# Token places in the rows, scattered block results, rows loaded by register address, and projections moved ahead of the dispatch

## The chip, the cores and the metric

The kernel runs on one core of a Trainium2 chip. The metric is the device time of one execution in microseconds (us); smaller is better. A core has TensorE (PE in the profile, its weight loads PEld), VectorE (DVE), ScalarE (ACT), GpSimd (POOL), SyncE (SP) and 16 DMA engines. On a profile's lines "L336" is line 336 of the kernel.

## The reference, cut to what matters

Three layers over x of 8 items, each 256 channels by 1024 positions, all in fp32:

```python
# layer 0: attention over each item's 1024 positions, 8 heads of 64, with a residual
qkv = (xt @ w_qkv + b_qkv).reshape(B, S, N_HEADS, 3 * D_K)
q, k, v = jnp.split(qkv, 3, axis=-1)
attn = softmax(einsum('bihd,bjhd->bijh', q, k) * SCALE, axis=1)   # over i, so each j is a column
res = einsum('bijh,bjhd->bihd', attn, v) @ w_out + b_out + xt
# layer 1: layer norm, then an attention of one head with one matrix W on the normed
#          tokens n (scores n W n^T, softmax, times n), added to the tokens
# layer 2: n = layer norm of the tokens; mixture of experts, 8 experts, the best 2 per token
probs = softmax(n @ router_w.T); rw, re = top_k(probs, 2); rw = rw / rw.sum(-1)
out = n
for e in range(8):
    h = gelu(n @ w1[e] + b1[e]); y = h @ w2[e] + b2[e]
    out = out + combine[:, e:e+1] * y      # combine holds rw at the chosen experts, else 0
# the tokens are added, and the result is returned as 8 x 256 x 32 x 32
```

A token's result therefore needs the rows of its two experts. The kernel computes only those, in sorted order.

## The kernel before, in words

**One item at a time.** For item b, `layer0` makes v for all positions (`values`, pv, L291) and q and k by head pair (`project`, pqk, L272, evicted by VectorE as qk, L280). It then runs 32 steps: four head pairs times eight column tiles. A step scores two heads on TensorE (psc, L323), takes the negative maximum on VectorE (nmax, L334), the exponential on ScalarE (ex, L336), scales the values on VectorE (rs L343, vs L345), and two steps later sums values on TensorE (po, L361). The next pair's projections are laid at column tiles 3 and 5. Then come the output projection (pr, L400 and L404) and t1 (L407). `attend` is the second layer: layer norm n1, transposes pt_n (L215), px (L421), scores ps (L436), transposes pa (L453), py (L458) and t2 (L463).

**Dispatch.** `dispatch` normalises t2 into n2, transposes it (pt_n, L215) and computes the router's scores pl (L482). Some 50 small VectorE operations choose the two best experts per token and count, with two small matmuls (pc L562, pn L564), at which row of its expert's region a token goes. For each 128 tokens and each of the two choices POOL then scatters 128 rows of 256 floats into `rows` in DRAM (L610): 16 indirect DMAs per item. POOL adds n2 to t2 (L617) and SP stores that as `sums` (L618).

The tiles n1, n2 and, later, `total` share the tag "n", which has one buffer: the next of them is written only when the last reader of the one before is done.

**Experts.** Items 0 to 6 are one group, item 7 is the second. When a group is dispatched, `plan` works out on VectorE which expert each block of 256 rows has, where its rows start (row_at), where its weights are (w_at) and at which place of y each token's two results will stand (yat). `experts` then runs 63 blocks for the first group, 15 for the second, in three staggered stages: `fetch` gathers weights (wb, L715, three buffers) and rows (xr, L724, three buffers) by POOL's indirect DMAs, and transposes the rows (px L733, xb L735); `hidden` is the first matrix and gelu (ph L743, hb L753); `collect` is the second matrix (pe L768), the bias (yb L777) and a store of the block to y by SP (L782).

**Results.** `results` loads an item's sums into `total` (o, L796), gathers for each 128 tokens the two rows of y by POOL (yk, L800, four buffers), adds them times their gates on VectorE (o, L806), transposes (pout, L817), copies on ScalarE and stores.

**Order.** The order on each engine is decided by a scheduler that goes by the order of the program and by what is ready in its own estimate; at run time each engine works in that fixed order. The program before:

```python
        for g in waiting:
            experts(g)
            for at, item in enumerate(g.items):
                between[at * NPAIR // len(g.items)].append((g, item))
        t1 = layer0(b, xT, between)
        t2 = attend(b, t1)
        dispatch(b, t2, group)
```

So the first group's blocks stand ahead of layer0(7), its results are spread between the head pairs of layer0(7), and experts(1) and results(7) end the kernel. At the start, while item 0 runs, SP fills `rows` with zeros and packs the weights (`prepare`).

Of the kernel before, what the change touches and what calls it, by code (L numbers as in the profile page):

```python
# [10 lines left out]
F32 = mybir.dt.float32  # L11
I32 = mybir.dt.int32
AF = mybir.ActivationFunctionType
ALU = mybir.AluOpType
AX = mybir.AxisListType
# [3 lines left out]
def kernel(  # L19
# [21 lines left out]
    nc = tc.nc  # L41
    P = 128
# [12 lines left out]
    BR = R * P  # L55
    WROW = NCC * FF + NFC * D + NFC + D
# [68 lines left out]
    for e in range(E):  # L125
# [15 lines left out]
    r_iota = const.tile([P, 1], F32, name="r_iota")  # L141
    nc.gpsimd.iota(
        r_iota, [[1, 1]], base=0, channel_multiplier=R, allow_small_or_imprecise_dtypes=True
# [74 lines left out]
    def prepare():  # L218

        zero = wbs[0][:, : 2 * D]  # L220
        with tc.issue_after(evicted[0, 0, 1].ins):
            nc.vector.memset(zero, 0.0)

        def fill(group):

            per = E * group.cap // (2 * P)
            return [
                nc.sync.dma_start(
                    group.rows.rearrange("(p c r) d -> p c (r d)", p=P, r=2)[:, c : c + 32],
                    zero.unsqueeze(1).to_broadcast([P, 32, 2 * D]),  # L230
                )
                for c in range(0, per, 32)
            ]

        first = fill(groups[0])[0]
        with tc.issue_after(first.ins):
            pack()
            for group in groups[1:]:
                fill(group)
# [62 lines left out]
    def layer0(b, xT, between):  # L302
# [4 lines left out]
        v = values(b, xT)  # L307
        res = one.tile([P, NPAIR, S], F32, tag="res", name=f"res_{b}")
        qks = [[project(b, xT, 0, t) for t in range(2)]]
        if b == 0:  # L310
            prepare()
# [61 lines left out]
        for at in range(last + LAG + 1):  # L373
            if at <= last:
                score(at, 0, 0)
            if 0 < at <= last + 1:
                score(at - 1, 1, 1)
                soften(at - 1, 1)
            if at <= last:
                score(at, 0, 1)  # L380
                score(at, 1, 0)
                soften(at, 0)
            if at >= LAG:
                gather_values(at - LAG)
            if at <= last:
                g, j = steps[at]
                if j == NT - 1:
                    for group, item in between[g]:
                        results(group, [item])
                if g + 1 < NPAIR and j in (3, 5):  # L390
                    if j == 3:
                        qks.append([])
                    qks[g + 1].append(project(b, xT, g + 1, len(qks[g + 1])))
# [17 lines left out]
    def attend(b, t1):  # L411
        n1 = one.tile([P, NT, D], F32, tag="n", name=f"n1_{b}")
# [64 lines left out]
    def gates(b, nT):  # L477

        pl = acc(f"pl_{b}")
        for i in range(NT):  # L480
            for dc in range(NCC):
                nc.tensor.matmul(  # L482
                    pl[:, ts(i, E)],
                    nT[:, dc, ts(i, P)],
                    rT[:, dc, :],
                    start=(dc == 0),
                    stop=(dc == NCC - 1),
                )

# [40 lines left out]
    class Group:  # L530


        def __init__(self, n, items):
            self.n, self.items = n, items
            self.cap = len(items) * S
            self.nb = 2 * self.cap // BR + E - 1
            self.rows = dram.tile([E * self.cap, D], F32, name=f"rows_{n}")
            self.views = dram_disjoint_views(self.rows, 2 * NT * len(items))
            self.y = dram.tile([self.nb * BR, D], F32, name=f"y_{n}")
            self.sums = [dram.tile([P, NT, D], F32, name=f"sums_{b}") for b in items]  # L540
            self.counts = None
            self.kept = {}
# [3 lines left out]
    def dispatch(b, t2, group):  # L546

        n2 = one.tile([P, NT, D], F32, tag="n", name=f"n2_{b}")
# [3 lines left out]
        gate, hots = gates(b, nT)  # L552
# [38 lines left out]
        kept = []  # L591
        for k in range(2):
# [3 lines left out]
            row = keep.tile([P, NT], F32, tag=f"row{k}", name=f"row{k}_{b}")  # L596
            nc.vector.tensor_reduce(row, sel, AX.X, ALU.add)  # L597
            nc.vector.tensor_mul(sel, hot, e_iota.unsqueeze(1).to_broadcast([P, NT, E]))
            exp = keep.tile([P, NT], F32, tag=f"exp{k}", name=f"exp{k}_{b}")
            nc.vector.tensor_reduce(exp, sel, AX.X, ALU.add)  # L600
            to = small.tile([P, NT], F32, tag="d_to", name=f"d_to_{b}_{k}", bufs=2)
# [3 lines left out]
            kept.append((row, exp, at))  # L605
        for i in range(NT):
            for k in range(2):
                at = kept[k][2]
                view = group.views[2 * (NT * group.items.index(b) + i) + k]
                nc.gpsimd.indirect_dma_start(  # L610
                    out=view[:, :],
                    out_offset=bass.IndirectOffsetOnAxis(ap=at[:, i : i + 1], axis=0),
                    in_=n2[:, i, :],
                    in_offset=None,
                )

        nc.gpsimd.tensor_add(t2, t2, n2)  # L617
        nc.sync.dma_start(group.sums[group.items.index(b)], t2)  # L618
        group.kept[b] = gate, [(row, exp) for row, exp, _ in kept]

    def plan(group):
# [23 lines left out]
        first = keep.tile([P, E], F32, tag="first", name=f"first_{n}", bufs=2)  # L645
# [7 lines left out]
        e_of = tmp("p_e", [nb])  # L653
# [10 lines left out]
        nc.vector.tensor_scalar(base, first, -float(BR), r_iota, ALU.mult, ALU.add)  # L664
# [5 lines left out]
        nc.vector.tensor_scalar_min(lo, lo, float(cap - R))  # L670
# [13 lines left out]


        for b in group.items:
            gate, kept = group.kept[b]
            ats = []
            for k, (row, exp) in enumerate(kept):
                hot = small.tile([P, NT, E], F32, tag="d_sel", name=f"p_hot_{b}_{k}", bufs=1)  # L690
                nc.vector.tensor_tensor(
                    hot,
                    exp.unsqueeze(2).to_broadcast([P, NT, E]),
                    e_iota.unsqueeze(1).to_broadcast([P, NT, E]),
                    ALU.is_equal,
                )
                nc.vector.tensor_mul(
                    hot, hot, first.unsqueeze(1).to_broadcast([P, NT, E])
                )
                to = small.tile([P, NT], F32, tag="d_to", name=f"p_to_{b}_{k}", bufs=2)  # L700
                nc.vector.tensor_reduce(to, hot, AX.X, ALU.add)
                nc.vector.scalar_tensor_tensor(to, to, float(BR), row, ALU.mult, ALU.add)
                at = keep.tile([P, NT], I32, tag=f"yat{k}", name=f"yat{k}_{b}")
                nc.vector.tensor_copy(at, to)
                ats.append(at)
            group.kept[b] = gate, ats
        return row_at, w_at

    def experts(group):
        n = group.n  # L710
        row_at, w_at = plan(group)

        def fetch(b):
# [9 lines left out]
            xr = rowp.tile([P, R, D], F32, tag="xr", name=f"xr_{n}_{b}")  # L723
            nc.gpsimd.indirect_dma_start(  # L724
                out=xr.rearrange("p r d -> p (r d)"),
                out_offset=None,
                in_=group.rows[:, :],
                in_offset=bass.IndirectOffsetOnAxis(ap=row_at[:, b : b + 1], axis=0),
# [7 lines left out]
            return xb  # L736

        def hidden(b, xb):
# [21 lines left out]
            return hT  # L760

        def collect(b, hT):
# [19 lines left out]
            nc.sync.dma_start(group.y[ts(b, BR), :].rearrange("(p r) d -> p r d", r=R), yb)  # L782

        line = [None, None]
        for b in range(group.nb + 2):
            if line[1] is not None:
                collect(*line[1])
            line[1] = (line[0][0], hidden(*line[0])) if line[0] is not None else None
            line[0] = (b, fetch(b)) if b < group.nb else None

    def results(group, items):
        for b in items:
            gate, ats = group.kept[b]
            sums = group.sums[group.items.index(b)]
            total = one.tile([P, NT, D], F32, tag="n", name=f"o_{b}")
            nc.sync.dma_start(total, sums)  # L796
            for i in range(NT):
                for k in range(2):
                    yk = four.tile([P, D], F32, tag="yk", name=f"yk{k}_{b}_{i}")
                    nc.gpsimd.indirect_dma_start(  # L800
                        out=yk[:, :],
                        out_offset=None,
                        in_=group.y[:, :],
                        in_offset=bass.IndirectOffsetOnAxis(ap=ats[k][:, i : i + 1], axis=0),
                    )
                    nc.vector.scalar_tensor_tensor(  # L806
                        total[:, i, :],
                        yk,
# [12 lines left out]

    waiting = []
    for b in range(B):
# [4 lines left out]

        between = [[] for _ in range(NPAIR)]
        for g in waiting:  # L830
            experts(g)
            for at, item in enumerate(g.items):
                between[at * NPAIR // len(g.items)].append((g, item))
        t1 = layer0(b, xT, between)
        t2 = attend(b, t1)
        dispatch(b, t2, group)
# [46 lines left out]
```

## Time and profile before

| what | value |
|---|---|
| median of 15 runs | 2924.97 us (2908.84 to 2943.03) |
| the profiled execution | 2926.14 us, span 2924.4 us |
| mean granted TensorE clock | 0.943 |
| TensorE matmuls | 2629.4 us, 90% |
| TensorE weight loads | 1373.6 us, 47% |
| VectorE | 1480.2 us, 51% |
| ScalarE | 844.1 us, 29% |
| POOL | 443.1 us, 15% |
| POOL's scatters of rows (L610) | 128, mean 977 ns |
| POOL's gathers: yk (L800), wb (L715), xr (L724) | 128 of 966 ns, 78 of 1015 ns, 78 of 963 ns |
| data moved by DMA | 209.17 MB |

The span is the time from the first to the last instruction of the profiled execution; its whole time is 1.7 us longer. Busy times are sums over the span, so an engine at 51% may still set the pace in one stage. A line of a timeline gives the start, the duration, the engine, the line, the operation with the tiles it writes and reads, and in brackets how long the engine stood idle before and what ended that. In the table of waits the three numbers are the total, the number of times and the longest, in us. In the table by stretches each row has the window, its length, the busy time and count for TensorE, its weight loads, VectorE, ScalarE and POOL, then the granted clock, the DMA share and GB/s.

### The profile page before, as it was taken

The page shows a single profiled execution, that of the slowest core. Times are in us where ns is not written, and L with a number is a line of the kernel's source. Part 1 is how long each engine was busy: PE and PEld are TensorE (multiplying, and loading weights), DVE is VectorE, ACT ScalarE, POOL GpSimd, SP SyncE. Part 2 cuts the span into 40 slices and gives each one's busy share as a digit, 9 for nine tenths or more (in the row PEclk, how much of TensorE's full clock was granted, in tenths as well). Part 3 has the DMA queues.
Part 4 walks back from the last instruction along what each step waited for, and adds up shares of the span by engine and source line. Part 5 has one row for each costly group of instructions (what it writes and reads, how often), then busy time and mean ns, then how long its engine had stood idle before and what let it go on. Part 6 is the DMA issues. An engine that isn't in the chain of part 4 may idle for free.

```text
span 2924.4 us, 26495 instructions
## 1 busy us (share of the span) xinstructions
PE 2629.4 (90%) x10049; PEld 1373.6 (47%) x10049; DVE 1480.2 (51%) x2666; ACT 844.1 (29%) x1451; POOL 443.1 (15%) x445
## 2 busy tenths in 40 slices
PE   8999999999999999999999998999499988878946
PEld 3346434633464346434643464346377752224634
DVE  4664566456645664565456545664433335545422
ACT  2531253125312531154125412531011113323101
POOL 0000200020002000200020002000444442441043
PEclk9999999999998999899999999999699998879968
DMA  6983100010001000100010001000355532332044
GB/s 246 385 301 127 58 1 15 1 44 1 15 1 44 1 15 1 43 1 15 0 44 1 15 0 44 1 1 1 121 176 186 183 98 80 111 94 69 0 169 156
DMA packets 89304, 209.17 MB, mean 72 GB/s; under 512 B 16256, under 2 KB 22040, under 8 KB 87128
## 3 DMA queue, kind: packets, MB, share of 16 engines
q1 hardware_dynamic: 59272, 128.87, 12.1%
q0 software_dynamic: 29904, 78.61, 8.4%
q8 instruction: 79, 1.29, 0.2%
q14 instruction: 49, 0.40, 0.0%
HBM read 113.22 MB, written 126.36 MB: 82 GB/s over the span
## 4 chain that ended last, share of the span: by engine, by line
PE 73%; issue 16%; DVE 6%; ACT 3%; DMA 2%; POOL 1%; another core or an unknown queue 0%; ACTq 0%; SPq 0%; DVEq 0%; POOLq 0%
PE psc L323 18%; PE po L361 15%; PE py L458 8%; PE ps L436 7%; PE pqk L272 6%; PE pr L400 4%; PE pe L768 3%; PE ph L743 2%; PE pt_n L215 2%; PE px L421 2%; PE pa L453 2%; PE pv L291 2%; DVE nmax L334 1%; ACT ex L336 1%; PE pl L482 1%
## 5 line engine op out<-in xcount | busy, mean ns | idle before, releaser
L336 ACT ACTIVATE ex<-psc,nmax 128x1024 f32<-128x1024 f32 x512 | 570.7, 1115 | 880.3 <-DVE nmax L334 729.1
L334 DVE TENSOR_REDUCE nmax<-psc 128x1 f32<-128x1024 f32 x512 | 604.1, 1219 | 261.6 <-PE psc L323 222.8
L323 PE MATMUL psc<-qk,qk 64*128 64x512 f32 x2048 | 615.9, 642 | 48.9 <-DVE qk L280 25.7
L361 PE MATMUL po<-ex,vs 128*64 128x512 f32 x2048 | 513.2, 618 | 15.2 <-DVE vs L345 14.7
L323 PEld LDWEIGHTS psc<-qk,qk 64*128 64x128 f32 x2048 | 234.7, 190 | 396.6 <-ACT ex L336 171.2
L617 POOL TENSOR_TENSOR t<-t,n 128x2048 f32<-128x2048 f32 x8 | 36.1, 4511 | 1907.9 <-issue 1500.3
L361 PEld LDWEIGHTS po<-ex,vs 128*64 128x64 f32 x2048 | 128.0, 138 | 371.6 <-issue 308.3
L272 PE MATMUL pqk<-xT,wqkv 128*128 128x512 f32 x512 | 239.5, 614 | 12.5 <-ACT ex L336 10.7
L458 PE MATMUL py<-n,aT 128*128 128x256 f32 x1024 | 236.5, 384 | 11.2 <-DVE aT L455 11.2
L436 PE MATMUL ps<-nT,xa 128*128 128x512 f32 x512 | 236.8, 592 | 0.0
L458 PEld LDWEIGHTS py<-n,aT 128*128 128x128 f32 x1024 | 190.4, 190 | 67.4 <-DVE aT L455 43.8
L280 DVE TENSOR_SCALAR qk<-pqk,b_qk 128x1024 f32<-128x1024 f32 x64 | 82.2, 1284 | 200.1 <-PE pqk L272 191.7
L272 PEld LDWEIGHTS pqk<-xT,wqkv 128*128 128x128 f32 x512 | 95.6, 194 | 156.5 <-issue 110.7
L768 PE MATMUL pe<-wb,hb 128*128 128x256 f32 x624 | 155.2, 392 | 13.6 <-ACT hb L753 8.4
L447 ACT ACTIVATE ex<-ps,nmax 128x1024 f32<-128x1024 f32 x64 | 71.3, 1115 | 332.8 <-DVE nmax L444 325.1
L800 POOL DMA_INDIRECT yk<-y,yat x128 | 123.7, 966 | 204.1 <-DVE o L806 109.1
L743 PE MATMUL ph<-xb,wb 128*128 128x256 f32 x624 | 151.4, 386 | 3.2 <-DVE xb L735 3.1
L610 POOL DMA_INDIRECT rows<-n,d_at x128 | 125.0, 977 | 170.5 <-DVE row L597 118.4
L753 ACT ACTIVATE hb<-ph,wb 128x256 f32<-128x256 f32 x156 | 65.5, 471 | 282.0 <-issue 241.1
L463 DVE SCALAR_TENSOR_TENSOR t<-py,rs,t 128x256 f32<-128x256 f32 x64 | 31.0, 484 | 228.2 <-PE py L458 228.2
L291 PE MATMUL pv<-wqkv,xT 128*128 128x512 f32 x256 | 135.0, 677 | 9.0 <-ACT wqkv L95 7.2
L735 DVE COPY xb<-px 128x512 f32<-128x512 f32 x78 | 54.0, 692 | 157.0 <-PE px L733 101.0
(151 smaller groups left out, 2332.9 us busy)
## 6 DMA issues: line engine op xcount, KB each, us to landing
rows<-wb SPq DMA_DIRECT2D x8, 8192.0 KB
y<-yb SPq DMA_DIRECT2D x78, 256.0 KB
sums<-t SPq DMA_DIRECT2D x8, 1024.0 KB
o<-sums SPq DMA_DIRECT2D x8, 1024.0 KB
out_dram<-oT SPq DMA_DIRECT2D x16, 512.0 KB
xT<-in_x_dram SPq DMA_DIRECT2D x7, 1024.0 KB
wpack<-in_L_ffn_w_dram SPq DMA_DIRECT2D x4, 1024.0 KB
rows<-n,d_at POOLq DMA_INDIRECT x128
```

The costliest lines, as they stand in the source:

```text
L272: nc.tensor.matmul(pq[:, ts(n, 512)], wqkv[:, cc, t, ts(g, P)], xT[:, cc, ts(n, 512)], start=(cc == 0), stop=(cc == NCC - 1),)
L291: nc.tensor.matmul(pv[:, ts(j, 512)], xT[:, cc, ts(i + j, P)], wqkv[:, cc, 2, :], start=(cc == 0), stop=(cc == NCC - 1),)
L323: nc.tensor.matmul(pss[at, h][:, ts(n, 512)], k[r, ts(j, P)], q[r, ts(n, 512)], start=True, stop=True)
L334: nc.vector.tensor_reduce(nmax, ps, AX.X, ALU.max, negate=True)
L336: nc.scalar.activation(ex, ps, AF.Exp, bias=nmax, scale=1.0, accum_out=sums[at][:, h : h + 1])
L361: nc.tensor.matmul(po[n][h * DK : (h + 1) * DK, :], vs[:, h, :], exs[h][:, ts(n, 512)], start=(j == 0), stop=(j == NT - 1),)
L436: nc.tensor.matmul(psc[:, ts(n, 512)], xa[:, ec, ts(i, P)], nT[:, ec, ts(n, 512)], start=(ec == 0), stop=(ec == NCC - 1),)
L458: nc.tensor.matmul(py[:, :D], aT[:, ts(m, P)], n1[:, m, :], start=(m == 0), stop=(m == NT - 1))
L610: nc.gpsimd.indirect_dma_start(out=view[:, :], out_offset=bass.IndirectOffsetOnAxis(ap=at[:, i : i + 1], axis=0), in_=n2[:, i, :], in_offs ...
L743: nc.tensor.matmul(ph[:, ts(fc, BR)], wb[:, dc * FF + fc * P : dc * FF + (fc + 1) * P], xb[:, dc, :], start=(dc == 0), stop=(dc == NCC - 1),)
L768: nc.tensor.matmul(py[:, ts(r, D)], hT[:, fc, ts(r, P)], wb[:, at + fc * D : at + (fc + 1) * D], start=(fc == 0), stop=(fc == NFC - 1),)
L800: nc.gpsimd.indirect_dma_start(out=yk[:, :], out_offset=None, in_=group.y[:, :], in_offset=bass.IndirectOffsetOnAxis(ap=ats[k][:, i : i + ...
```

## The change

Four things are changed together.

1. A row in `rows` is 260 floats, not 256: column 256 holds the token's place (2 * token, within the group), column 257 its first expert, the last two are zero. Empty rows have 2^22 in the place's column. The tiles with tag "n" become 260 wide.
2. y is indexed by token, two rows each. A block computes on VectorE where each of its rows goes: the place, plus one if the block's expert is the row's first. POOL scatters the block in two indirect DMAs with a bounds check that drops empty rows. `results` then loads 128 tokens' two rows with one plain load of 256 KB on SP (yk in two buffers), and `plan` no longer computes yat.
3. A block's rows are loaded by SP with a plain DMA whose address is read into a register from row_at, not gathered by POOL.
4. `values` and the first projections of the next item are a function of their own, `begin`, called after the router's matmuls and ahead of the rest of the dispatch. The first group's experts stand between layer0(7) and attend(7), and its results after dispatch(7); nothing is laid between the head pairs of layer0(7).

```diff
+    RW = D + 4
+    NOWHERE = float(2**22)
...
-    def layer0(b, xT, between):
-        v = values(b, xT)
-        res = one.tile([P, NPAIR, S], F32, tag="res", name=f"res_{b}")
+    def begin(b, xT):
+        v = values(b, xT)
         qks = [[project(b, xT, 0, t) for t in range(2)]]
         if b == 0:
             prepare()
+        return v, qks
...
-                if j == NT - 1:
-                    for group, item in between[g]:
-                        results(group, [item])
...
+        nc.vector.tensor_scalar_add(
+            rows2[:, :, D : D + 1], t_iota.unsqueeze(2), float(2 * S * item)
+        )
...
+            if k == 0:
+                nc.vector.tensor_copy(rows2[:, :, D + 1 : D + 2], exp.unsqueeze(2))
+                nc.vector.memset(rows2[:, :, D + 2 : RW], 0.0)
...
-                    in_=n2[:, i, :],
+                    in_=rows2[:, i, :],
...
-            xr = rowp.tile([P, R, D], F32, tag="xr", name=f"xr_{n}_{b}")
-            nc.gpsimd.indirect_dma_start(
-                out=xr.rearrange("p r d -> p (r d)"),
-                out_offset=None,
-                in_=group.rows[:, :],
-                in_offset=bass.IndirectOffsetOnAxis(ap=row_at[:, b : b + 1], axis=0),
+            with tc.issue_after(loads[-1]) if loads else nullcontext():
+                row = nc.sync.value_load(
+                    row_at[0:1, b : b + 1], min_val=0, max_val=E * group.cap - BR
+                )
+            xr = rowp.tile([P, R, RW], F32, tag="xr", name=f"xr_{n}_{b}")
+            load = nc.sync.dma_start(
+                xr, group.rows[bass.ds(row, BR), :].rearrange("(p r) d -> p r d", r=R)
+            )
+            loads.append(load.ins)
+            to = small.tile([P, R], I32, tag="y_to", name=f"y_to_{n}_{b}")
+            nc.vector.scalar_tensor_tensor(
+                to.unsqueeze(2),
+                xr[:, :, D + 1 : D + 2],
+                e_of[:, b : b + 1],
+                xr[:, :, D : D + 1],
+                ALU.is_equal,
+                ALU.add,
             )
...
-            nc.sync.dma_start(group.y[ts(b, BR), :].rearrange("(p r) d -> p r d", r=R), yb)
+            for r in range(R):
+                nc.gpsimd.indirect_dma_start(
+                    out=group.y_views[R * b + r][:, :],
+                    out_offset=bass.IndirectOffsetOnAxis(ap=to[:, r : r + 1], axis=0),
+                    in_=yb[:, r, :],
+                    in_offset=None,
+                    bounds_check=2 * group.cap - 1,
+                    oob_is_err=False,
+                )
...
+            places = group.y.rearrange("(i p k) d -> i p k d", p=P, k=2)
             for i in range(NT):
+                yk = two.tile([P, 2, D], F32, tag="yk", name=f"yk_{b}_{i}")
+                nc.sync.dma_start(yk, places[NT * item + i])
                 for k in range(2):
-                    yk = four.tile([P, D], F32, tag="yk", name=f"yk{k}_{b}_{i}")
-                    nc.gpsimd.indirect_dma_start(
...
+    begun = begin(0, next_x)
...
+        t1 = layer0(b, xT, *begun)
         for g in waiting:
             experts(g)
-            for at, item in enumerate(g.items):
-                between[at * NPAIR // len(g.items)].append((g, item))
-        t1 = layer0(b, xT, between)
         t2 = attend(b, t1)
-        dispatch(b, t2, group)
+        normed = norm_tokens(b, t2)
+        if b + 1 < B:
+            begun = begin(b + 1, next_x)
+        dispatch(b, *normed, group)
+        for g in waiting:
+            results(g, g.items)
         waiting = [group] if b == group.items[-1] else []
```

`norm_tokens` holds the layer norm, the transposes and the router's matmuls that stood at the head of `dispatch`.

## The prediction

> **What bounds the kernel now.** I read the shares and the chain first.
>
> ```profile
> PE 2629.4 (90%) x10049; PEld 1373.6 (47%) x10049; DVE 1480.2 (51%) x2666; ACT 844.1 (29%) x1451; POOL 443.1 (15%) x445
> PE 73%; issue 16%; DVE 6%; ACT 3%; DMA 2%; POOL 1%; another core or an unknown queue 0%; ACTq 0%; SPq 0%; DVEq 0%; POOLq 0%
> ```
>
> TensorE sets the time; what can be won is where it idles. The waits of TensorE and the table by stretches (busy time by engine, granted clock, DMA share, GB/s) say where:
>
> ```profile
> PE px L733 <- DMA xr<-rows,row_at: 65.1, 2, 33.4
> PE pout L817 <- DVE o L806: 33.6, 16, 7.7
> ...
> 292.90:507.70 214.80, 206.49 (x773) 89.02 (x773) 128.58 (x228) 81.19 (x140) 20.19 (x17) 0.96 0.07 25
> 2048.00:2099.00 51.00, 12.17 (x52) 10.33 (x52) 27.16 (x139) 1.97 (x3) 26.24 (x23) 0.52 0.29 109
> 2099.00:2376.50 277.50, 265.16 (x1263) 218.89 (x1264) 86.48 (x125) 54.19 (x127) 118.66 (x121) 0.99 0.52 171
> 2373.70:2699.10 325.40, 264.69 (x841) 103.60 (x839) 165.40 (x293) 97.33 (x155) 108.33 (x112) 0.85 0.29 89
> 2791.10:2822.90 31.80, 0.07 (x2) 0.04 (x1) 6.16 (x46) 1.28 (x1) 21.68 (x22) 0.50 0.39 143
> 2822.90:2892.40 69.50, 65.03 (x300) 52.74 (x300) 20.06 (x29) 12.60 (x30) 23.62 (x24) 0.96 0.62 213
> 2892.40:2924.40 32.00, 5.53 (x17) 2.30 (x16) 8.45 (x17) 1.93 (x2) 15.32 (x16) 0.56 0.33 107
> ```
>
> The first row is a plain item, pt_n of one item to attend's px of the next: full. Rows two to four are routing of item 6, the 63 blocks, and layer0(7), where the results of items 0 to 6 are laid between head pairs and TensorE idles 61 (325.4 - 264.7). Rows five to seven are the tail. TensorE's timeline at the first gap:
>
> ```profile
> 2047.96 3.92 PE L215 MATMUL pt_n<-ident,n 128*128 128x128 f32 x16 [2.48 <-DVE n L206]
> 2064.99 0.63 PE L564 MATMUL pn<-d_both,ones 128*128 128x64 f32 x2
> 2099.04 1.11 PE L733 MATMUL px<-ident,xr 128*128 128x128 f32 x4 [33.41 <-DMA xr<-rows,row_at]
> ```
>
> TensorE stands from pn to px while VectorE routes, POOL issues 16 scatters and they land. At items 1 to 6 there is no such gap: the next item's pv already lies between pl and pc, so there the new order fills nothing.
>
> **Change, the front.** From pt_n of item 6 (2048.0) to px of attend(7) (2699.1) before takes 651.1. After, the same stretch is a plain item plus 63 blocks. The six plain items take 214.8, 215.5, 217.3, 219.4, 215.0 and 212.5, mean 215.75; px of neighbouring blocks are 4.335 apart, so 273.1. Together 488.9: 162.2 less. It holds the 33.4 wait and the 113 by which the interleaved results stretch layer0(7).
>
> **Change, item starts.** VectorE's order has gates still ahead, but the second half of the routing, 18 small operations of dispatch (0.25 each), behind the next projections' evictions. VectorE's timeline at the start of item 1's heads, and POOL's first scatters in the tail:
>
> ```profile
> 329.38 3.49 DVE L334 TENSOR_REDUCE nmax<-psc 128x1 f32<-128x1024 f32 x3 [2.07 <-PE psc L323]
> ```
>
> ```profile
> 2794.20 1.01 POOL L610 DMA_INDIRECT rows<-n,d_at  x1 [11.66 <-DVE row L597]
> 2798.17 0.97 POOL L610 DMA_INDIRECT rows<-n,d_at  x1 [0.30 <-issue]
> ```
>
> Nine of the 18 fall before the first nmax, under its wait of 2.07; nine fall between it and the second, 2.1, and behind them on VectorE stand nmax, for which the exponentials and then TensorE's next scores wait. Moving pc and pn ahead of the scores saves TensorE's 0.45 gap: 1.7 each, 10 for six starts (bounds 0, if the three score buffers cover it, and 27, all 18 uncovered).
>
> In item 7 the first three y_to operations stand on VectorE behind vs of step 2, with every later nmax queued behind them, and they need rows that SP loads only when all 16 scatters of item 6 have landed. By item 1's clock (pt_n at 292.9) that slot comes at 344.5, 51.6 after pt_n. The routing ends at the second nmax, 36.5 + 1.2 + 2.1 = 39.8 after pt_n; 16 scatters at 1.28 are 20.5, their landing and the load 2.25 each: 64.8 to 66. So about 14 of stall (bounds 0, if the scheduler's place is loose, and 24, if plan's 20 operations come in between and three loads run one by one). The rest of plan(0) lies under the scatters.
>
> **Change, blocks.** Removed: a POOL gather of rows (0.96). Added: two scatters, a register read and an issue on SP, one y_to. POOL per block: three at 1.29 (the weights' gather has a bounds check too) is 3.9, under 4.335. SP's issue is 0.33 to 0.77 and hides under the block; y_to (bounds 0.15 to 0.48, rows of small and 256-wide operations) hides in VectorE, which is busy 86 of 277. So zero. Below nothing lies at most the 12 that TensorE idles in the 63 blocks (277.5 - 265.2). Above: if POOL stands each block until yb is written (0.69) and one more issue gap (0.30), a block is 4.9, and 78 cost 44. I take zero, since POOL's row at this pitch leaves 0.4.
>
> For the register read no row exists. The Trainium skill ("DMA: Bandwidth & Descriptors", Latency and other measured facts) gives a floor of about 0.6 us; by it nothing here changes.
>
> Rows of 1040 bytes no longer sit on 256. The weights' rows, 5128 bytes, do not either, and move 213 GB/s at a share of 0.62, 344 at a full share; the zero fill with 2048 byte pieces moves 345 at 0.95, 363. So at most 5% in the fill, which ends at 225 where its first reader comes at 294.
>
> The same page (How a descriptor splits into AXI transactions) speaks against such rows: a piece that starts off a 256-byte boundary fetches unused bytes. By its count a 1040-byte piece can need a sixth transaction; an estimate of up to 20% on scatters, still under POOL's pitch, so the time is the same.
>
> **Change, the tail.** After pn of item 7 (2791.1) before takes 133.3. After, results of items 0 to 6 stand there first, and 100 of their 112 transposes are ahead of block 0 on TensorE. Their `total` shares one buffer (tag n) with n2 of item 7, so the load of sums waits for its scatters. These begin 3.1 after pn as before and 16 at 1.28 take 20.5; with landing, 25. The load's price is a row of the chain of waits, from the last transpose to VectorE:
>
> ```profile
> 2449.23 6.70 DMA o<-sums
> ```
>
> Bounds are 4.3 (256 KB stored and released in 2.25, the other 0.79 MB at the best slice's 385 GB/s) and 6.7. I take 5.9, near the row, since it is the same transfer without the gathers that ran beside it.
>
> Each item reads eight 256 KB tiles through two buffers. Two are fetched ahead: four multiply-adds of 0.48, 1.93. Then each pair costs one load, 2.25 (the store's time, the nearest row), and the two multiply-adds of the tile that frees the next, 0.96: 3.2, three times 9.6. That is 11.5. Between items the last transposes (0.8) release `total`, and its load (5.9) is alone: 18.2.
>
> Sum: 25 + 5.9 + 11.5 + 6 x 18.2 = 151.6; rest of the transposes among the blocks 3; blocks 60.3 (as before from 2832 to 2892.4). Then results(7): bias add 0.8, one scatter pitch 1.3, landing 2.9 (issue to VectorE of a gather), load 2.25, 11.5, and 6.7 from the last multiply-add to the end: 25.4, where 32.0 was. Tail 240.3, 107 more.
>
> SP's queue now holds, in order, per item six tile loads, the next item's first two, its sums, and two stores; row loads of group 1 stand behind them and cost at most one load, 2.25, which the 3 above cover.
>
> Off the path: 128 gathers of y leave POOL and plan's places leave VectorE; dispatch gains an add, a copy and a memset, 0.25 each. They lie under VectorE's waits (42 for pl in all); uncovered, 0.75 at each of eight items, 6. The x load that begin needs is issued an item earlier, as before.
>
> **Sum.** Span 2924.4 - 162.2 + 10 + 14 + 107 = 2893.2; the run was 1.7 longer than its span (2926.1) and 1.2 over the median (2925.0): 2894.
>
> **Rivals.** *Results slower.* The 8 tiles of an item load one at a time, not two: each costs 2.25 + 0.96, an item 9.6 more, eight items 77: 2971. For it: one SP queue, a single `total` buffer, and the old results made TensorE wait for o 16 times (33.6). Against: loads of different tiles need no common buffer. It decides from 22 us per item (31 of gain over eight items, 3.9 on 18.2). Chance 0.17.
>
> *Blocks paced by POOL.* 4.9 each, 44 more: 2938. For: 3.9 of 4.335, and in POOL's order the scatters, which wait for VectorE, stand ahead of the next weights' gather, whose data TensorE needs. Against: POOL's pitch stays at 1.3 in the rows, and yb is VectorE's first work after pe. It decides from 4.73 a block (31 of gain over 78). Chance 0.15.
>
> *No stall, quick loads.* y_to and the starts cost nothing (-24), sums at 4.3 (-11): 2859. Chance 0.13.
>
> That the change does not do what it says is part of the forecast: filled routing brings nothing at six of seven items; the gain is item 7's.
>
> **How the numbers follow.** Forecast 0.55, own range 2872 to 2918. Measurement tells about 0.3%, 9 us: faster is below 2916, slower above 2934. The forecast has 0.49 faster, 0.05 same, 0.01 slower; quick loads are faster; POOL gives 0.05 same and 0.10 slower; slow results 0.17 slower. The range, 2855 to 2948, takes in quick loads and paced blocks and leaves out most of the slow results (0.17).
>
> **What would show it.** Right: no wait of px in layer0(7)'s neighbourhood, blocks 4.3 apart, seven results of 18 in a row after item 7 with TensorE idle, y_to waiting 10 to 20 in item 7. Wrong: an item of results over 22 or under 14, blocks over 4.6, or item starts that lose more than 4.

## The result, and the profile after

The changed kernel took 3002.58 us (median of 9 runs, 2997.28 to 3015.12) where the kernel before took 2925.29 (46 runs): a ratio of 1.0275, interval 1.0253 to 1.0297. The forecast was 2894 and the range ended at 2948. The profiled execution took 3003.0, with a span of 3001.3.

The same program was then run on three more chips (numbers 12, 2 and 10 on record), on which the kernel before took 2899 to 2901. The record does not number the chip of the first runs; "first chip" below means that chip at that hour, and "second chip" is number 12. There it took 2907.35 (ratio 1.0024, interval 1.0014 to 1.0034), 2903.26 (1.0013, 1.0002 to 1.0024) and 2909.45 (1.0030, 1.0013 to 1.0046). So two things have to be explained: a loss of 3 to 10 where 31 of gain was forecast, and some 70 more on the first chip.

By stages, from the traces (us; on the second chip both kernels were profiled side by side):

| stage | forecast | first chip, before to after | second chip, before to after |
|---|---|---|---|
| pt_n of item 0 to pt_n of item 6 | +10 | 1755.1 to 1801.3: +46 | 1733.1 to 1730.2: -3 |
| pt_n of item 6 to pt_n of attend(7) | -162 + 14 | 647.1 to 527.4: -120 | 636.3 to 501.5: -135 |
| pn of item 7 to the end | +107 | 133.3 to 282.0: +149 | 135.6 to 284.7: +149 |

The page of the changed kernel, its waits of TensorE and of VectorE, and its table by stretches (same columns as before), first chip:

```profile
PE 2636.2 (88%) x10049; PEld 1375.3 (46%) x10049; DVE 1486.7 (50%) x2690; ACT 842.5 (28%) x1450; POOL 401.4 (13%) x395
```

```profile
PE pout L837 <- DVE o L826: 161.6, 53, 37.6
PE psc L333 <- DVE qk L286: 52.0, 15, 14.0
```

```profile
DVE o L826 <- DMA o<-sums: 87.0, 7, 30.9
DVE qk L286 <- remote: 52.7, 6, 8.9
DVE y_to L738 <- DMA xr<-rows: 33.9, 21, 12.7
DVE xb L751 <- remote: 29.5, 7, 5.6
DVE yb L793 <- remote: 5.3, 2, 3.1
```

```profile
591.70:814.70 223.00, 211.82 (x772) 89.75 (x772) 128.88 (x229) 81.26 (x140) 20.10 (x17) 0.94 0.05 20
2093.50:2325.30 231.80, 212.97 (x784) 91.29 (x785) 132.77 (x253) 83.53 (x144) 23.32 (x20) 0.93 0.08 29
2325.30:2625.60 300.30, 265.02 (x1252) 215.41 (x1250) 97.38 (x187) 53.23 (x125) 186.93 (x185) 0.99 0.47 147
2719.40:2755.60 36.20, 0.00 (x0) 0.00 (x0) 5.21 (x37) 0.00 (x0) 18.64 (x19) 0.50 0.46 162
2755.60:2895.35 139.75, 32.38 (x96) 14.55 (x97) 46.27 (x103) 12.84 (x13) 0.00 (x0) 0.50 0.58 181
2895.35:2975.40 80.05, 68.68 (x316) 54.06 (x316) 28.65 (x55) 14.53 (x32) 40.89 (x41) 0.96 0.61 195
```

What the reader is to see: the wait of px for rows is gone from TensorE's list, as forecast. In its place stands pout waiting for o, 161.6. A plain item (first row) takes 223.0 where 212.5 to 219.4 stood. The fourth and fifth rows are the new tail: 36.2 in which TensorE does nothing, then 139.75 for six periods of results, in which TensorE, VectorE and ScalarE are all mostly idle and the DMA share is 0.58: a chain, not a busy engine.

For the waits put down to "remote" the trace shows no program step that ended them. On VectorE of the first chip they are 22.6 before (nmax 18.0, qk 4.6) and 87.5 after (52.7 + 29.5 + 5.3); ScalarE has 18.9 more after. They are idle time, part of which would have passed anyway, and not yet lateness. On the second chip neither kernel has one. One of them, in the timelines of TensorE, VectorE and POOL of the first chip:

```profile
643.06 3.70 PE L278 MATMUL pqk<-xT,wqkv 128*128 128x512 f32 x8
653.63 2.07 PE L333 MATMUL psc<-qk,qk 64*128 64x512 f32 x2 [4.96 <-DVE qk L286]
```

```profile
652.29 1.28 DVE L286 TENSOR_SCALAR qk<-pqk,b_qk 128x1024 f32<-128x1024 f32 x1 [8.79 <-remote]
```

```profile
648.76 0.97 POOL L635 DMA_INDIRECT rows<-n,d_at  x1 [0.30 <-issue]
```

By TensorE's records pqk was done at 646.8. VectorE was free from 643.5 and started qk at 652.29: 5.5 of the 8.79 are late, and the start is 2.56 after POOL was done issuing the last of the item's 16 scatters (649.73). In the trace three completion signals of TensorE, for matmuls that by the records ended up to 2 us apart, came within 0.11 us just before. Six items show it at the same place, 2.5 to 2.6 after the last scatter. In each of them the step between the second pair's two projections takes 19.8 where the second chip has 11.8.

The kernel before has such places on the first chip too. There the scatters come earlier, and at four of its items a late maximum starts 2.5 to 2.7 after the last of them. One, on VectorE and POOL:

```profile
1803.47 2.36 DVE L334 TENSOR_REDUCE nmax<-psc 128x1 f32<-128x1024 f32 x2 [4.13 <-remote]
```

```profile
1799.88 0.97 POOL L610 DMA_INDIRECT rows<-n,d_at  x1 [0.30 <-issue]
```

### The profile page after: what moved, and what is told of

Its sections match the earlier page's. It is cut to its first block, busy times and chain, and to the rows that moved or that the text cites. A ratio compares the mean times of both kernels' runs of the same rounds, so it can differ in the third digit from the quotient of the medians.

```text
span 3001.3 us, 26962 instructions
## 1 busy us (share of the span) xinstructions
PE 2636.2 (88%) x10049; PEld 1375.3 (46%) x10049; DVE 1486.7 (50%) x2690; ACT 842.5 (28%) x1450; POOL 401.4 (13%) x395
## 4 chain that ended last, share of the span: by engine, by line
PE 70%; issue 16%; DVE 6%; ACT 3%; another core or an unknown queue 2%; DMA 2%; POOL 2%; ACTq 0%; POOLq 0%; SPq 0%; DVEq 0%
PE psc L333 15%; PE po L371 14%; PE py L465 8%; PE ps L443 7%; PE pqk L278 6%; PE pv L297 5%; PE pr L407 3%; PE pe L784 3%; PE px L428 2%; PE pt_n L218 2%; PE ph L759 2%; PE pa L460 2%; DVE nmax L344 1%; PE pl L489 1%
## 5 line engine op out<-in xcount | busy, mean ns | idle before, releaser
L333 PE MATMUL psc<-qk,qk 64*128 64x512 f32 x2048 | 598.8, 636 | 62.5 <-DVE qk L286 52.0
L465 PE MATMUL py<-n,aT 128*128 128x256 f32 x1024 | 236.6, 384 | 11.2 <-DVE aT L462 11.2
L799 POOL DMA_INDIRECT y<-yb,y_to x156 | 154.4, 990 | 448.3 <-DVE yb L793 368.8
L837 PE MATMUL pout<-ident,o 128*128 128x128 f32 x128 | 41.9, 434 | 161.6 <-DVE o L826 161.6
L297 PE MATMUL pv<-wqkv,xT 128*128 128x512 f32 x256 | 146.9, 731 | 8.9 <-ACT wqkv L97 7.2
```

The source lines that it names most:

```text
L297: nc.tensor.matmul(pv[:, ts(j, 512)], xT[:, cc, ts(i + j, P)], wqkv[:, cc, 2, :], start=(cc == 0), stop=(cc == NCC - 1),)
L333: nc.tensor.matmul(pss[at, h][:, ts(n, 512)], k[r, ts(j, P)], q[r, ts(n, 512)], start=True, stop=True)
L465: nc.tensor.matmul(py[:, :D], aT[:, ts(m, P)], n1[:, m, :], start=(m == 0), stop=(m == NT - 1))
L799: nc.gpsimd.indirect_dma_start(out=group.y_views[R * b + r][:, :], out_offset=bass.IndirectOffsetOnAxis(ap=to[:, r : r + 1], axis=0), in_= ...
```

## The experiments

**The changed kernel again, and the kernel before again** (the program as it is).

> The changed kernel once more, as it is, beside a second profile of the kernel before. In its first profile TensorE's completion signals stood 5.5 late at the second head pair of each item. In three kernels that leave the items as they are, run on another chip, that hold was gone (items of 287 to 288, not 300). Theory A (the hold belongs to the chip or to the hour, not to the program): items are 287 to 292 here too and the time is about 2915. Theory B (it belongs to the program as built, and each of the edits happened to end it): items are 300 and the time is 2980 or more.

> The kernel before, once more with a profile, so that the stages of both are seen on one chip. All theories: blocks of 4.33, px waiting 33 and 32 for rows; items of 289 to 293; only the clock's dips may lie elsewhere.

> The changed kernel a third time, to see whether late completion signals of TensorE come again. Where they do (waits put down to remote, 87 in its first profile), items take 300 and the time is near 3000; where they do not, items take 288 and the time is 2907. Either way it is the base for the two kernels beside it.

> The changed kernel on another occasion. If TensorE's late completion signals show again: items of 300 and about 3000. If not: items of 288 and about 2905.

2907.35, 2897.68 (one run), 2903.26 and 2909.45. Items take 288.4 in the changed kernel and 288.9 in the kernel before, in the mean of six, and no wait is put down to remote. So the late signals belong to the first chip or its hour, with this program: theory A. On the second chip a changed item still starts with 10.9 from first score to first po where 8.1 to 9.2 stood, the 1.7 forecast; in turn its stretch from pt_n to the first score shows a granted clock of 0.94 (29.8 and 30.8 long) where the kernel before has 0.85 (34.4 long), and the two cancel.

**The dispatch ahead of the projections.**

```diff
-        if b + 1 < B:
-            begun = begin(b + 1, next_x)
         dispatch(b, *normed, group)
+        if b + 1 < B:
+            begun = begin(b + 1, next_x)
```

> The changed kernel with one thing undone: the whole dispatch of an item stands ahead of the next item's projections again. An item takes 300.3 us in the changed kernel and 292.5 before. Theory (the later routing puts the 16 scatters, 38 to 58 us after pt_n, over the projections of the second head pair, whose completion TensorE signals only when the last scatter has landed): items return to 292 to 294, the wait of y_to in item 7 (10.6) goes as well since the rows come 16 earlier, and the time is 3002 - 46 - 10 = 2946. Rival (the wider n tiles, the extra dispatch operations or the granted clock lengthen the items): items stay at 298 or more and the time stays above 2985.

> The dispatch ahead of the next item's projections, beside the changed kernel. If the late signals show: theory (the scatters lie over the second pair's projections) 293 an item and 45 less than the changed kernel beside it; rival (the clock, the wider rows) 298 or more. If they do not show: the same time as the changed kernel within 10.

2911.36 (ratio to the kernel before 1.0045, interval 1.0029 to 1.0062) and 2917.79 (1.0061, 1.0036 to 1.0086), beside 2909.45 of the changed kernel in the second call. The items take 289.1 and 289.6. No signal was late on these chips, so the theory was not put to the test. What it shows is that the new order of projections and routing by itself is worth about 8 at most, and that item 7's stall on y_to does not go with it, against the expectation (the second pair's projections start 64.4 after pt_n there, 49.3 in the other items).

**Dense total.**

```diff
-            total = one.tile([P, NT, RW], F32, tag="n", name=f"o_{b}")[:, :, :D]
+            wide = one.tile([P, NT, RW], F32, tag="n", name=f"o_{b}")
+            total = wide.rearrange("p i d -> p (i d)")[:, : NT * D].rearrange(
+                "p (i d) -> p i d", d=D
+            )
```

> The changed kernel with one thing changed: total in the results lies dense in its buffer (2048 floats a partition in a row) and not in rows 260 floats wide; the same single buffer and order. Theory (the load of sums is slow because its pieces are 1024 bytes, 46 ns each on an engine, about 200 GB/s): from the last transpose of an item to the first multiply-add of the next 8.6 falls to 5 to 6, an item from 23.1 to 20, and with eight items the time falls by 20 to 25 to about 2980. Rival (the load waits behind the prefetched tiles and the two stores in SP's one queue): an item stays within 1 of 23.1.

2894.12 (0.9978, interval 0.9966 to 0.9991), 10 to 15 under the changed kernel by the ratios. An item's period falls from 22.8 (second chip) to 21.5, and the wait for sums in the periods from 8.8 to 7.4. Half of the expectation: 1024-byte pieces cost about 1.4 an item (1.1 to 1.5 beside the other kernels of the same call, which leave the results' order and tiles alone and take 22.6 to 23.0). The queue costs less: by the DMA records on the first chip the two prefetched tiles still move for 1.5 after sums is issued, and its own first packet starts 1.3 to 1.5 after issue, where 0.95 stood in the kernel before. The two stores of the item before run beside the load in both kernels.

**Blocks stored by SP.**

```diff
-            for r in range(R):
-                nc.gpsimd.indirect_dma_start(
-                    out=group.y_views[R * b + r][:, :],
...
+            nc.sync.dma_start(group.y[ts(b, BR), :].rearrange("(p r) d -> p r d", r=R), yb)
```

> The changed kernel with POOL's two scatters per block replaced by one plain store by SP to the block's own place in y; the results read as many bytes from y, so they add the wrong rows. Theory (TensorE's completion signals come late, 1.5 to 5.6 us, while scatters to memory are under way; 32 us over the 63 blocks and 8 over the 15): every block is 4.33 again, the time falls by 35 to 45 to about 2962. Rival (SP's load with a register address, whose issue waits for the transposes of three blocks before, or its landing sets the late blocks): blocks of 5 to 7.7 remain and the time changes by less than 10.

2882.12 (0.9930, interval 0.9888 to 0.9973). From the second of the first group's 63 blocks on, the steps from pe to pe exceed 4.335 each by 1.2 in sum, against 8.9 in the changed kernel on the second chip and 30.1 on the first (9.4 and 8.7 in the two kernels above on this run's own chip). The waits of TensorE in the 63 blocks, changed kernel on the second chip:

```profile
PE pe L784 <- ACT hb L769: 10.9, 60, 0.5
PE ph L759 <- DMA wb<-wpack,w_at: 4.6, 5, 1.7
```

With the plain store the first is again 10.9 and the second is gone. So the scatters do slow the blocks, by 8; 4.6 of it is the wait for the weights' gather, which stands behind them on POOL. The 15 blocks at the end are as late as ever (10.3 over; 10.9 in the changed kernel), so there it is not the scatters. In the kernel with two buffers, below, they are 3.2 over: most of this lateness goes with the results in front of them. Of the rest of the gain, results(7) here need only 8 of the 15 blocks and start before the last, which the expectation had not counted.

**Half the scatters of rows.**

```diff
-            for k in range(2):
+            for k in range(1):
                 view = group.views[2 * (NT * item + i) + k]
```

> The changed kernel with only the first of each token's two rows scattered (8 indirect DMAs an item, not 16; y is filled once at the start, and the other row's result is missing); the order of the program is the same, so are the routing's operations on VectorE. Theory (TensorE's signals are held until the scatters have landed): the scatters end about 48 us after pt_n, ahead of the next projections at 51.4, so the 5.5 hold on qk goes and an item takes 293 to 296; y_to's wait in item 7 goes too (10.6): the time is 2950 to 2965. Rival (the 18 routing operations in front of the first maxima, or the lower granted clock that follows the late start, cost the 7.7): items stay at 299 to 300 and only y_to's wait goes: 2990.

> Half the scatters of rows, same order, beside the changed kernel (the second row of each token is left out). If the late signals show: theory 293 to 296 an item, rival 299 or more. If they do not show: items of 288 as in the changed kernel and 20 to 25 less in all, from the earlier rows in item 7 and in the tail.

2884.45 (0.9953, interval 0.9925 to 0.9981) and 2885.09 (0.9943, 0.9909 to 0.9977). Items take 289, as without the edit (288.0 to 289.1). In item 7 the step between the two projections of the second pair is 19.6 and 20.6, not 28.0 to 28.6, and the first result begins 25.8 and 26.4 after pn, not 36.7: both wait for the landing of the scatters. On the late signals it says nothing, since none came.

**Later y_to.**

```diff
-            nc.vector.tensor_copy(xb.rearrange("p c t -> p (c t)"), px[:, : NCC * BR])
+            copied = nc.vector.tensor_copy(xb.rearrange("p c t -> p (c t)"), px[:, : NCC * BR])
+            to = small.tile([P, R], I32, tag="y_to", name=f"y_to_{n}_{b}")
+            with tc.issue_after(copied.ins):
+                nc.vector.scalar_tensor_tensor(
...
```

> The changed kernel with y_to of each block issued after the copy xb of the same block, and so no longer among the first maxima of layer0(7). Theory (the first three y_to stand on VectorE ahead of a maximum and wait for rows that come 13 to 16 later): the step between the projections of pairs 1 and 2 in item 7, 28.3 in the changed kernel, is 11.8 like in every other item, and the time falls by 15 to 17. Rival (plan's operations or the scatters hold VectorE there): the step stays above 20 and less than 5 is gained.

2891.12 (0.9966, interval 0.9951 to 0.9981), 12 less than the changed kernel of the same call where 15 to 17 were expected. The step, which by the program is the one between the two projections of the second pair (the expectation calls it pairs 1 and 2), is 11.8, and from pt_n of item 6 to pt_n of attend(7) it is 485.7. The stall that it ends, in VectorE's timeline of the changed kernel on the second chip:

```profile
2069.58 0.29 DVE L355 TENSOR_TENSOR vs<-v,rs 128x128 f32<-128x128 f32 x1
2082.61 0.22 DVE L738 SCALAR_TENSOR_TENSOR y_to<-xr,e_of 128x2 int32<-128x2 f32 x1 [12.74 <-DMA xr<-rows]
2086.89 0.22 DVE L738 SCALAR_TENSOR_TENSOR y_to<-xr,e_of 128x2 int32<-128x2 f32 x1 [4.06 <-DMA xr<-rows]
2087.03 1.28 DVE L286 TENSOR_SCALAR qk<-pqk,b_qk 128x1024 f32<-128x1024 f32 x1
```

The second load lands 4 after the first, and a projection's eviction stands behind it: 16.5 of stall in TensorE's step, between the forecast's 14 and its bound of 24.

**Two buffers for the results.**

```diff
-            total = one.tile([P, NT, RW], F32, tag="n", name=f"o_{b}")[:, :, :D]
+            total = two.tile([P, NT, D], F32, tag="xT", name=f"o_{b}")
...
-                yk = two.tile([P, 2, D], F32, tag="yk", name=f"yk_{b}_{i}")
-                nc.sync.dma_start(yk, places[NT * item + i])
+            yk = one.tile([P, NT, 2, D], F32, tag=("res", "v")[item % 2], name=f"yk_{b}")
+            nc.sync.dma_start(
+                yk,
+                group.y[2 * S * item : 2 * S * (item + 1), :].rearrange(
...
```

> The changed kernel with the results' loads taken off the single buffers: total in the two buffers of xT, dense, and an item's eight tiles of y by one 2 MB load into res and v in turn (all free by then). The results still stand in a row after dispatch(7). Theory (an item of results is a chain: last transposes, load of sums, tiles in pairs): it ends, an item costs 8 (16 multiply-adds of 0.485) to 11.2 (4 MB of loads and stores at about 370 GB/s), nothing waits for the scatters, and 23 a time falls to 8 to 12: 80 to 120 less than the changed kernel of the same chip. Rival (VectorE or the transposes on a slow clock set the item): an item stays above 15 and less than 60 is gained.

2788.45 (0.9613, interval 0.9592 to 0.9634), 119 less than the changed kernel in the same call, at the top of the 80 to 120 expected. The edit changes three things at once (two buffers for `total`, its dense shape, one load of y for eight), and the 119 is not split among them; the dense shape alone gave 10 to 15. VectorE's timeline at two items of results in the changed kernel on this chip, then its timeline in this one, and the table by stretches of this one from pn to the first ph of the last 15 blocks:

```profile
2703.76 1.67 DVE L826 SCALAR_TENSOR_TENSOR o<-yk,gate,o 128x256 f32<-128x256 f32 x4 [8.85 <-DMA o<-sums]
2707.80 1.92 DVE L826 SCALAR_TENSOR_TENSOR o<-yk,gate,o 128x256 f32<-128x256 f32 x4 [2.37 <-DMA yk<-y]
...
2726.79 1.67 DVE L826 SCALAR_TENSOR_TENSOR o<-yk,gate,o 128x256 f32<-128x256 f32 x4 [9.02 <-DMA o<-sums]
```

```profile
2540.31 0.88 DVE L830 SCALAR_TENSOR_TENSOR o<-yk,gate,o 128x256 f32<-128x256 f32 x2 [2.99 <-DMA yk<-y]
...
2627.26 0.47 DVE L830 SCALAR_TENSOR_TENSOR o<-yk,gate,o 128x256 f32<-128x256 f32 x1
```

```profile
2623.90:2687.20 63.30, 23.48 (x85) 13.74 (x84) 37.95 (x120) 7.86 (x9) 29.35 (x19) 0.50 0.91 335
```

The chain is gone, and not only by quicker items. With their buffers free, the multiply-adds of items 0 and 1 already stand among those of attend(7), from 2540.31, 84 ahead of pn, and attend(7) takes 82.9 where it took 80.8. Only items 2 to 6 are left behind pn: the first of them begins 3.4 after it, and the stretch of 63.3 runs at a DMA share of 0.91. Now the transfers set them. These five take 6.6 to 17.8 each, 11.8 in the mean, just above the theory's 8 to 11.2; with seven items in the row the gain would have been smaller.

**Results within attend(7)**, one item between two of its steps, with the same buffers.

```diff
             pending = now
+            if ready and i:
+                results(ready[0], [ready[1].pop(0)])
```

> The same with the results of items 0 to 6 laid between the steps of attend(7), one item a step, where VectorE is busy 3 of 10 us. Theory: only TensorE's 16 transposes an item (3.5 each, 25 in all) remain of them, and the tail is that of the kernel before: 110 to 150 less than the changed kernel. Rival (3 MB a step compete with nothing there but VectorE's fixed order makes attend wait for landings, as between the head pairs before): attend(7) grows by 60 or more and the gain is less than the one of the two buffers alone.

2797.73 (0.9647, interval 0.9631 to 0.9663): the tail is 129.9, but attend(7) grows from 80.8 to 122.9, and px waits 29.1 for rows again. It lies between theory and rival, 9 above the version that keeps five of the seven items in a row behind pn, where their transfers cover that very wait.

**Both**, two buffers and later y_to.

> The two buffers for the results and the later y_to together. Theory: the two gains add, 119 and 16: 2772 where the kernel before takes 2901, 4.4% less. Rival (the blocks that start without the wait only wait for weights or rows): 2785 to 2790.

2773.59 (0.9561, interval 0.9548 to 0.9574): the gains add, and this beats both kernels, by 126 and 130. A single row of its table, from pt_n of item 6 to pt_n of attend(7):

```profile
2022.40:2509.30 486.90, 464.55 (x2009) 299.03 (x2010) 225.74 (x436) 134.63 (x265) 207.81 (x203) 0.99 0.34 107
```

## Why the prediction was wrong

On the first chip the changed kernel's span is 108 longer than forecast: 42 in the tail, 36 in the items and 28 in the stretch from item 6 to attend(7). On the second chip, against the kernel before there, the tail is again 42 over; the items are 13 under the forecast, and the stretch gains 13 less, mostly because the kernel before itself takes 10.9 less for it there.

**Step that failed on every chip: the price of an item of results.** The mechanism was the forecast's (seven items in a row, one after the other, TensorE idle), the size was not. The term was 18.2; it measured 23.1 on the first chip and 22.8 on the second. Of the 4.9, the load of sums took 2.7 (8.6 from the last transpose to the first multiply-add, against 5.9, and above the bound of 6.7). 0.8 of it is the step from the row's 6.7 down to 5.9, taken because gathers were said to run beside the row's load, from 2449.23 to 2455.93. None did; POOL in the kernel before:

```profile
2456.78 0.96 POOL L800 DMA_INDIRECT yk<-y,yat  x1 [51.62 <-DVE o L806]
```

The row's load was also one of a dense tile with an empty queue ahead of it, while here `total` is a slice of a 260-wide tile, loaded in 1024-byte pieces (about 1.4, shown by dense total), behind two tiles (about 0.5, by its first packet). The other 2.2 are the multiply-adds: 13.7 from first to last against 11.5, a pair 3.5 to 4.0, not 3.2, because 2.25 was the time of a store and a tile's load took 2.7 (issue at 2779.36, multiply-add at 2782.09). Six periods make 29. The start of the results was 36.2 after pn and not 30.9: the first load of sums was issued at 24.8, as forecast, but took 11.4 to the first multiply-add, with the weights' gathers for the last blocks moving beside it. The stretch from the last item's start through the blocks was 81.4, not 74.8, with the 15 blocks 8 late. Tail: 282 and not 240.

The forecast gave the point itself: from 22 an item the results decide. They took 23. The rival that named that point had another mechanism, tiles loaded one at a time; the tiles did come in pairs. With the measured tail the forecast's sum comes to 11 more than the kernel before; 3 to 10 more was measured where no signal was late.

**Blocks at no cost.** 9 late over the first group's blocks on the second chip, 30 on the first; within the bound of 44, but not zero. The plain store shows 8 of the 9 to be the scatters, more than half of it by way of the weights' gather behind them on POOL: the rival's mechanism at a fifth of its price. The 21 more on the first chip come with late starts there: xb, yb and hb begin up to 4.4 after TensorE's records say that their input was done.

**Item starts, +10.** Without late signals the routing's operations cost what was forecast, and the clock gave it back. On the first chip the term became +46, beyond the bound of 27. No step of the forecast had the cause: TensorE's completion signals come late there while scatters are under way, and the change moves the scatters from 22 to 42 after pt_n to 38 to 58 after it, onto the second pair's projections (51.4). That the late signals make most of the difference, the steps say: the six items take 71 more than on the second chip, and 48 of that are the step between the second pair's projections (8.0 each), into which the late qk falls. The kernel before loses 22 in its items there, with its own late maxima. That the scatters' place makes the signals late was not shown by an experiment, because no later chip had the effect. It rests on the times alone: 2.5 to 2.6 after the last scatter in all six items, and 2.5 to 2.7 at four items of the kernel before, whose scatters lie elsewhere. Its mechanism stays open.

**What held.** The front: with the y_to stall taken away, 490.4 to 491.5 from pt_n of item 6 to px of attend(7), forecast 488.9 (a plain item and 63 blocks). The wait of px is gone. The y_to stall, by the named order on VectorE: 16.5 against 14 (9 on the first chip, where item 7 was late already). The filling of the routing brings next to nothing: items 288.4 and 288.9. The last results: 25.9 against 25.4. Unaligned rows: the scatters' pitch stayed at 1.28.

**The two rules that were weighed.** The register read (the Trainium skill, "DMA: Bandwidth & Descriptors", Latency and other measured facts: a floor of about 0.6 us) is 0.27 as an instruction on SP in the first chip's trace (median of 78; 0.34 on the second, where the shortest is 0.26 and the longest 1.20), and SP has 0% of the chain that ended last. The extra transactions of unaligned pieces (the Trainium skill, the same page, How a descriptor splits into AXI transactions) do not show in the scatters: a 4160-byte packet takes 180 ns where a 4096-byte one took 186. The prediction's count was off as well: rows at multiples of 1040 bytes start on multiples of 16, so by the page's rule, as an estimate, such a row takes five transactions where an aligned 1024-byte one takes four, and never a sixth.

## What to carry to other kernels

When work is taken from between other work and set in a row, price it as a chain: every single-buffered tile in it puts a whole transfer on the path, with the queue that stands ahead of that transfer and with the piece size that the tile's shape gives. Look for buffers that are free by then; here they were worth 119, where the whole change was forecast to gain 31; part of that came because two of the seven items could then be done earlier. And a small operation whose input lands late goes after the work that needs nothing, not where the scheduler finds room.

## What the runs showed of the hardware

TensorE's completion signals reached VectorE several us late (5.5 to 5.6 at six places, up to 4.4 in the blocks) around POOL's scatters, on one chip and not on three others with the same program; there the kernel before is some 25 slower and the changed one some 95. A comparison on one chip was therefore 2.75% where three others gave 0.1 to 0.3%.
